# Two-layer convolution and attention kernel: the first residual's additions as accumulating on-chip transfers issued from GpSimd

## The chip, the cores and the metric

The kernel runs on one core of a Trainium2 chip. The metric is the device time of one execution in microseconds (us), lower is better. The engines are called as the profile calls them: PE (TensorE, matrix products), DVE (VectorE), ACT (ScalarE), POOL (GpSimd) and SP (SyncE, which here only issues transfers). Each takes its instructions in the order in which they were issued to it and waits on semaphores for the others.

## The reference: what is computed

The input is 16 images of 256 channels and 56 x 56 pixels, float32. Two layers follow one another, each added to its own input:

```python
# layer 0
x = x + _L0_conv_ref(_gn(x), ...)
# layer 1
x = x + _L1_conv_ref(_gn(x), ...)
```

`_gn` normalizes groups of 8 channels of an image to mean 0 and variance 1. Layer 0 takes the sign of that, makes three grouped 3 x 3 convolutions (4 groups of 64 channels, dilations 1, 3 and 5) with binarized weights, scales and rectifies each one, sums the three, and normalizes the sum over the 256 channels of each pixel. Layer 1 projects to queries, keys and values (8 heads of 8 channels), lets each pixel attend to its 3 x 3 neighbours with a learned and a fixed part, and projects back to 256 channels. The addition that the change touches is the first of the two `x + ...`.

## The kernel before

**Tiling.** An image's 28 upper and 28 lower rows lie side by side on 2 x 64 partitions for the signs. For everything after the convolutions an image is worked on in two strips, `u` 0 and 1. A strip has a tile for each of the four channel groups `g`: 128 partitions (two quarters of the rows x 64 channels) of 2 x 392 pixels, float32, so 784 elements or 3136 bytes per partition. `ct[g]` holds the group's layer-0 result, and `xt` holds the strip of the input, all four groups, and becomes the output in place.

**One strip of layer 0.** `conv` (L634) makes 36 products per group and dilation on PE (L644); ACT (L663, L670, L678), DVE (L673, L683) and POOL (L689) scale, rectify and sum them in `ct[g]`. `load_unit` (L1196) loads `xt` by four transfers from SP's queue (L1202). `channel_norm` (L721) follows: ACT squares (L727), PE sums over channels (L697) and spreads mean and root back (L711), DVE subtracts the mean (L755) and scales (L765), which also sums the result per partition. Then come the lines that the change is about, four times per strip, once per group: L778 adds `ct[g]` to `xt[:, g]`, and ACT's L782 squares the sum and collects the squares per partition in `sums`; it writes the squares over `ct[g]`.

**After both strips.** `fold` (L794) takes the statistics of the sum, from which layer 1's normalization follows: six small products on PE (L514, the group of that line with six products), some DVE and ACT steps, four POOL multiplications of the query, key and value weights (L803) and eight PE products (L825). Then `qkv` (L856) multiplies `xt` by these weights (L862), and `scores` (L906) and `attend` (L975) make the attention of each strip: POOL makes nine products per strip of queries and shifted keys (L915), PE sums them (L937), DVE and ACT and POOL make the softmax (L950 to L972), PE spreads it (L986), DVE multiplies with shifted values (L997), POOL adds these up (L1010, L1015 on DVE for the last), PE projects back (L1027), DVE adds to `xt` (L1037), and SP stores the strip (L1047).

**The next image's signs** are made meanwhile: SP loads each group twice into one of three `xh` buffers (L544), once for the statistics on ACT (L570) and once for the sign (L594); their statistics go through another L514, with two products. SP also copies 5 rows of signs across the two halves within the chip (`sgn<-sgn`, L606 and L607).

**What sets the order.** The program doesn't run these steps as they are written down. Each is an `Op` with the buffers it reads and writes; `Plan.emit` (L351) issues them by a hand-kept table of due times (`ORDER`, L80), one number per step and stage, with a period of 126.77 per image, as soon as the steps they depend on have been issued and a buffer is free. Steps of neighbouring images are so interleaved in every engine's queue. `either` (L492) puts a step on POOL, or on DVE where the table `ON_VECTOR` (L280) names it; for L778 that is so for three steps of the last image (stage `scale1$`). `pool` (L486) always puts it on POOL. Both count as one step, so that the due times of all steps stay with their steps. The buffers that matter here: 3 of `xt`, 7 of `ct`, 3 of `xh`, 3 of `m` (L1010), 5 of `p` (L915).

Of the kernel before, what the change touches and what calls it, by code (L numbers as in the profile page):

```python
# [11 lines left out]
ALU = mybir.AluOpType  # L12
# [281 lines left out]
class Plan:  # L294
# [16 lines left out]
    def op(self, engine, emit, r=(), w=(), hold=(), engines=()):  # L311


        k = self.noted.get((self.stage, self.image), 0)
        self.noted[self.stage, self.image] = k + 1
        if engines:
            emit = partial(emit, engines[k in ON_VECTOR.get(self.stage, ())])
        bufs = [k[0] if isinstance(k, tuple) else k for k in (*r, *w, *hold)]
        bufs = [k for k in dict.fromkeys(bufs) if isinstance(k, Buf)]
        o = Op(PERIOD * self.image + ORDER[self.stage][k], emit, bufs)  # L320
        for b in bufs:
            if not b.left and b.kind in self.queues:
                self.queues[b.kind].append(b)
            b.left += 1
        before = {}
        for k in r:
            for x in self.wrote.get(k, ()):
                before[id(x)] = x
        for k in w:
            for x in (*self.wrote.get(k, ()), *self.read.get(k, ())):  # L330
                before[id(x)] = x
        for k in r:
            self.read.setdefault(k, []).append(o)
        for k in w:
            self.wrote[k], self.read[k] = [o], []
        for x in before.values():
            x.after.append(o)
            o.wait += 1
        self.ops.append(o)
# [35 lines left out]
def preact_conv_attention(  # L375
# [16 lines left out]
    nc = tc.nc  # L392
# [84 lines left out]
    def pe(f, r, w, hold=()):  # L477
        op("PE", f, r, w, hold)

    def act(f, r, w):  # L480
        op("ACT", f, r, w)

    def dve(f, r, w):
        op("DVE", f, r, w)

    def pool(f, r, w):  # L486
        op("POOL", f, r, w)
# [4 lines left out]
    def either(f, r, w):  # L492

        op("POOL", f, r, w, engines=(nc.gpsimd, nc.vector))
# [199 lines left out]
    def lanes_sum(ps, bank, src, g):  # L694

        for i in range(NVB):
            nc.tensor.matmul(  # L697
                out=ps[i * LANES : (i + 1) * LANES, bank, 0:VB],
                lhsT=cm32,
                rhs=src[:, i // 2, i % 2 * VB : (i % 2 + 1) * VB],  # L700
                start=g == 0,
                stop=g == NG - 1,
            )

    def lanes_spread(ps, src):


        def f():
            for e in range(2):
                for h, q in ((0, 0), (1, 1), (0, 1), (1, 0)):  # L710
                    nc.tensor.matmul(  # L711
                        out=ps[q * GC : (q + 1) * GC, h, e * VB : (e + 1) * VB],
                        lhsT=bsel[e][q][h * GC : (h + 1) * GC],
                        rhs=src[h * GC : (h + 1) * GC, 0:VB],
                        start=True,
                        stop=True,
                    )

        pe(f, [src], [ps])

    def channel_norm(b, u, ct, xt, sums):  # L721

        ps = Buf("ps")
        for g in range(NG):
            plan.at(f"var{u}", b)
            sq = Buf("sq")
            act(lambda g=g, sq=sq: nc.scalar.activation(sq.tile, ct[g].tile, AF.Square), [ct[g]], [sq])  # L727

            def sum_of_both(g=g, sq=sq):
                lanes_sum(ps, 0, ct[g], g)  # L730
                lanes_sum(ps, 1, sq, g)

            pe(sum_of_both, [ct[g], sq], [ps])
        plan.at(f"root{u}", b)
        ms, t, s, r = (Buf("lv") for _ in range(4))


        mean, square = (lambda i=i: ps[:, i, 0:VB] for i in range(2))
        tt = nc.vector.tensor_tensor
        stt = nc.vector.scalar_tensor_tensor  # L740
        act(lambda: nc.scalar.copy(ms.tile, mean()), [ps], [ms])
        dve(lambda: tt(t.tile, mean(), ms.tile, ALU.mult), [ps, ms], [t])
        dve(lambda: stt(mean(), t.tile, -1.0, square(), ALU.mult, ALU.add), [t], [ps])
        dve(lambda: nc.vector.tensor_scalar(mean(), mean(), 0.0, EPS_LN, ALU.max, ALU.add), [], [ps])
        act(lambda: nc.scalar.activation(t.tile, mean(), AF.Ln), [ps], [t])
        act(lambda: nc.scalar.activation(square(), t.tile, AF.Exp, scale=-0.5), [t], [ps])
        act(lambda: nc.scalar.activation(s.tile, square(), AF.Square, scale=0.5**0.5), [ps], [s])
        dve(lambda: stt(t.tile, mean(), -1.0, s.tile, ALU.mult, ALU.mult), [ps, s], [t])
        dve(lambda: stt(r.tile, t.tile, 1.5, square(), ALU.add, ALU.mult), [t, ps], [r])
        plan.at(f"mean{u}", b)  # L750
        mb = Buf("ps")
        lanes_spread(mb, ms)
        for g in range(NG):
            dve(
                lambda g=g: nc.vector.tensor_tensor(ct[g].tile, ct[g].tile, mb[:, :, 0:SN], ALU.subtract),  # L755
                [mb],
                [ct[g]],
            )
        plan.at(f"root{u}", b)
        rb = Buf("ps")  # L760
        lanes_spread(rb, r)
        for g in range(NG):
            plan.at(f"scale{u}", b)
            dve(
                lambda g=g: nc.vector.scalar_tensor_tensor(  # L765
                    ct[g].tile,
                    ct[g].tile,
                    gam[:, g : g + 1],
                    rb[:, :, 0:SN],
                    ALU.mult,  # L770
                    ALU.mult,
                    accum_out=sums[:, g : g + 1],
                ),
                [rb],
                [ct[g], (sums, "sums")],
            )
            either(
                lambda e, g=g: e.tensor_tensor(xt[:, g], xt[:, g], ct[g].tile, ALU.add),  # L778
                [ct[g]],
                [(xt, g)])  # L780
            act(
                lambda g=g: nc.scalar.activation(  # L782
                    ct[g].tile,
                    xt[:, g],
                    AF.Square,
                    bias=bet[:, g : g + 1],
                    accum_out=sums[:, NG + g : NG + g + 1],
                ),
                [(xt, g)],
                [(sums, "squares"), ct[g]],  # L790
            )
# [420 lines left out]
    for b in range(NB):  # L1212
        sums = []
        xts = []
        for u in range(NU):
            ct = [Buf("ct") for _ in range(NG)]
            for g in range(NG):
                for d in range(3):
                    plan.at(f"conv{u}", b)
                    conv(b, u, g, d, ct[g])  # L1220
            plan.at(f"load{u}", b)
            xts.append(load_unit(b, u))
            sums.append(Buf("g"))
            channel_norm(b, u, ct, xts[u], sums[-1])
        before = sx
        if b + 1 < NB:
            sx = signs(b + 1)
        plan.at("fold", b)
        wf, bf = fold(before, sums)
        for u in range(NU):  # L1230
            for j in range(3):
                plan.at(f"qkv{u}", b)
                qkv(b, xts[u], wf, bf, j, u)
        for u in range(NU):
            at = scores(b, u)
            attend(b, u, at, xts[u])
# [114 lines left out]
```

## Time and profile before

| What | Value |
|---|---|
| Median of two runs | 2101.8 us (2094.55 and 2109.05) |
| The profiled execution | 2101.32 us |
| Its span, first to last instruction | 2099.5 us |
| Granted TensorE clock, mean | 0.935 of full speed |
| PE / DVE / ACT / POOL busy | 1798.0 / 1625.2 / 1292.8 / 1508.4 us |
| DMA engines, share of the span | 45.0% for SP's queue, 211.68 MB |
| L778 on POOL | 125 additions, 240.1 us, median 1.86 us |
| L778 on DVE | 3 additions, median 1.06 us |
| L782 on ACT | 128 squares, 121.1 us, idle before them 42.0 us |

How to read it. The page of a profile is one execution on the chip. "Busy" is the time in which an engine worked; instructions that only issue a transfer or wait are not counted in it. A group of instructions has a row of its own: the line of the program, engine, operation, what it writes `<-` what it reads, shapes, count `x`, then busy time in us and the mean of one in ns, then the time that the engine stood idle just before such instructions and what ended it (the releaser). The chain of work that ended last is followed back from the end, each time to what released an instruction. A timeline row has start and length in us, engine, line, operation, tiles, shapes and count, and in square brackets an idle time before it with its releaser. A row of the DMA issues ends with the size of a transfer and the median time from the start of its issue to its landing. A row of the waits gives who waited for whom, the total in us, how often, and the longest. Images and strips are counted from 0; from one image to the next the timeline advances by some 121 us (the first squares of the second strip start at 901.05, 1023.48, 1143.02 and 1265.15 us in images 6 to 9).

### The profile page before, as it was taken

Reading aid. Unit: us, or ns where it says so; the run is one execution under the profiler, and the core shown is the slowest. Engines: PE = TensorE matmul, PEld = TensorE weight load, DVE = VectorE, ACT = ScalarE, POOL = GpSimd, SP = SyncE. Lnnn points to the kernel's source line nnn. Section 1 sums busy time; section 2 is a strip of 40 time slices with the busy share of each in tenths; the row PEclk is TensorE's granted clock in tenths of the full one; section 3 lists DMA queues with packets and bytes.
Section 4 is the critical chain, followed back from the end, with each engine's and each line's share of the span. In section 5 each row is a group of like instructions: output and inputs, shape, how many; then the busy total and the mean of one; then the engine's idle time right before and its main releaser. Section 6 shows DMA issues by size and latency. Waiting matters only on the chain.

```text
span 2099.5 us, 71196 instructions
## 1 busy us (share of the span) xinstructions
PE 1798.0 (86%) x31770; PEld 906.3 (43%) x31770; DVE 1625.2 (77%) x2240; ACT 1292.8 (62%) x1733; POOL 1508.4 (72%) x884
## 2 busy tenths in 40 slices
PE   5667799898989989898989989898998989899694
PEld 4444254353535445353534435353443535344241
DVE  7565696968788696878879697877969687796876
ACT  6785575667667565767666576775757677463310
POOL 2233968878796887879597777968788786977714
PEclk8879999899999999999999999999999999999886
DMA  6760435535363654536364452637455353232212
GB/s 167 171 137 18 97 81 130 126 80 131 80 143 83 141 113 94 127 73 139 82 146 108 105 129 68 136 77 167 87 112 130 83 122 90 60 65 63 63 32 62
DMA packets 102420, 216.24 MB, mean 103 GB/s; under 512 B 10720, under 2 KB 84832, under 8 KB 102112
## 3 DMA queue, kind: packets, MB, share of 16 engines
q1 hardware_dynamic: 102112, 211.68, 45.0%
q8 instruction: 249, 4.08, 0.8%
q14 instruction: 59, 0.48, 0.1%
HBM read 154.85 MB, written 51.38 MB: 98 GB/s over the span
## 4 chain that ended last, share of the span: by engine, by line
PE 48%; DVE 27%; ACT 10%; issue 8%; POOL 4%; DMA 2%; SPq 0%; DVEq 0%; POOLq 0%; ACTq 0%
PE banks L644 16%; PE banks L862 12%; PE banks L937 7%; DVE m L997 5%; PE banks L986 4%; DVE xt L1037 4%; ACT xh L570 4%; PE banks L697 4%; DVE ct L765 3%; DVE ct L683 2%; ACT banks L678 2%; POOL m L1010 2%; DVE rl L683 2%; PE banks L1027 2%; DVE at L972 2%
## 5 line engine op out<-in xcount | busy, mean ns | idle before, releaser
L644 PE MATMUL banks<-sgn,wconv 64*64 64x392 bf16 x13824 | 674.3, 341 | 42.7 <-DVE rl L683 10.5
L1010 POOL TENSOR_TENSOR m<-m 128x784 f32<-128x784 f32 x252 | 469.7, 1864 | 169.1 <-DVE m L997 159.0
L644 PEld LDWEIGHTS <-wconv 64*64 64x64 bf16 x13824 | 441.5, 108 | 316.6 <-issue 144.4
L915 POOL TENSOR_TENSOR p<-qt,kt 128x784 f32<-128x784 f32 x273 | 473.1, 1768 | 108.8 <-PE banks L937 56.8
L678 ACT ACTIVATE banks<-banks,cbi,csc 128x784 f32<-128x784 f32 x384 | 373.0, 974 | 141.2 <-DVE ct L673 139.8
L689 POOL TENSOR_TENSOR ct<-ct,rl 128x784 f32<-128x784 f32 x128 | 237.9, 1859 | 247.0 <-DVE ct L683 99.9
L986 PE MATMUL banks<-at,wv 64*32 64x392 f32 x5120 | 315.6, 567 | 94.1 <-DVE m L997 49.9
L683 DVE SCALAR_TENSOR_TENSOR ct<-banks,oalpha,ct 128x784 f32<-128x784 f32 x256 | 262.0, 1028 | 84.9 <-ACT banks L678 82.7
L997 DVE TENSOR_TENSOR m<-banks,vt 128x784 f32<-128x784 f32 x288 | 274.6, 964 | 65.7 <-PE banks L986 59.3
L862 PE MATMUL banks<-xt,wf 64*64 64x392 f32 x3072 | 265.4, 495 | 3.9 <-DVE ct L755 3.9
L778 POOL TENSOR_TENSOR xt<-xt,ct 128x784 f32<-128x784 f32 x125 | 240.1, 1932 | 25.4 <-DVE ct L765 23.8
L937 PE MATMUL banks<-p,wk 32*64 32x392 f32 x4608 | 230.5, 499 | 11.7 <-POOL p L915 9.4
L673 DVE SCALAR_TENSOR_TENSOR ct<-banks,asc,ct 128x784 f32<-128x784 f32 x128 | 130.6, 1029 | 120.6 <-PE banks L644 117.1
L570 ACT ACTIVATE xh<-xh 128x1568 f32<-128x1568 f32 x120 | 180.9, 1508 | 7.2 <-DMA xh<-in_x 5.0
L986 PEld LDWEIGHTS banks<-at,wv 64*32 64x32 f32 x5120 | 67.3, 113 | 265.4 <-DVE m L997 106.1
L670 ACT ACTIVATE rl<-banks,asc 128x784 f32<-128x784 f32 x128 | 116.6, 911 | 103.6 <-POOL ct L689 59.1
L862 PEld LDWEIGHTS banks<-xt,wf 64*64 64x64 f32 x3072 | 114.3, 134 | 143.1 <-issue 131.0
L663 ACT ACTIVATE ct<-banks,mv,asc 128x784 f32<-128x784 f32 x128 | 128.3, 1003 | 49.1 <-PE banks L644 49.0
L683 DVE SCALAR_TENSOR_TENSOR rl<-banks,oalpha,rl 128x784 f32<-128x784 f32 x128 | 130.7, 1021 | 30.9 <-ACT banks L678 27.4
L1027 PE MATMUL banks<-m,wp 64*64 64x392 f32 x1024 | 116.2, 542 | 44.7 <-DVE xt L1037 24.7
L782 ACT ACTIVATE ct<-xt,pr 128x784 f32<-128x784 f32 x128 | 121.1, 947 | 42.0 <-POOL xt L778 34.3
L937 PEld LDWEIGHTS banks<-p,wk 32*64 32x64 f32 x4608 | 90.7, 131 | 118.4 <-issue 60.5
(111 smaller groups left out, 1961.8 us busy)
## 6 DMA issues: line engine op xcount, KB each, us to landing
xh<-in_x SPq DMA_DIRECT2D x248, 392.0 KB, 5.4
xt<-in_x SPq DMA_DIRECT2D x128, 392.0 KB, 7.0
out<-xt SPq DMA_DIRECT2D x128, 392.0 KB, 5.9
sgn<-sgn SPq DMA_DIRECT2D x128, 41.2 KB, 3.3
p<-in_w SPq DMA_DIRECT2D x12, 144.0 KB, 5.1
wq<-in_wqkv SPq DMA_DIRECT2D x1, 384.0 KB, 7.5
p<-in_wk_b SPq DMA_DIRECT2D x1, 320.0 KB, 6.9
p<-in_wk_c SPq DMA_DIRECT2D x1, 320.0 KB, 7.1
```

The costliest lines, as they stand in the source:

```text
L570: lambda func=func, col=col: nc.scalar.activation(inside(g) if b == 0 else image(xh), image(xh), func, accum_out=sums[:, col : col + 1]),
L644: nc.tensor.matmul(out=ps[q * GC : (q + 1) * GC, h, 0:SN], lhsT=wconv[h * GC : (h + 1) * GC, g, d, tap, :], rhs=sgn[g][h * GC : (h + 1) * ...
L678: lambda: nc.scalar.activation(n(), n(), AF.Relu, bias=cbi[:, g, s], scale=csc[:, g, s]),
L683: lambda: nc.vector.scalar_tensor_tensor(to.tile, n(), oalpha[:, g, s], to.tile, ALU.mult, ALU.add),
L689: lambda e: e.tensor_tensor(ct.tile, ct.tile, to.tile, ALU.add),
L778: lambda e, g=g: e.tensor_tensor(xt[:, g], xt[:, g], ct[g].tile, ALU.add),
L862: nc.tensor.matmul(out=ps[h * D : (h + 1) * D, q, 0:SN], lhsT=wf[q * GC : (q + 1) * GC, g, j, :], rhs=xt[q * GC : (q + 1) * GC, g, h, :], ...
L915: e.tensor_tensor(p.tile.rearrange("p x (r w) -> p x r w", w=W), _view(qt[:, 0, u * SN :], [(NU * SN + LANES, 2), (W, SR), (1, W)]), shift ...
L937: nc.tensor.matmul(out=ps[rt // 2][q * 64 : (q + 1) * 64, rt % 2, 0:n], lhsT=wk[r, j, :], rhs=rhs, start=s == 0, stop=s == 9,)
L986: nc.tensor.matmul(out=ps[rt * 32 : (rt + 1) * 32, q, 0:SN], lhsT=wv[q * 64 : (q + 1) * 64, j, :], rhs=at[q * 64 : (q + 1) * 64, rt, 0:SN] ...
L997: lambda j=j, m=m, ps=ps: nc.vector.tensor_tensor(m.tile.rearrange("p x (r w) -> p x r w", w=W), _view(ps[:, 0, :], [(512, 2), (W, SR), (1 ...
L1010: lambda e, m=m, acc=acc: e.tensor_tensor(acc.tile, acc.tile, m.tile, ALU.add),
```

## The change

In `channel_norm`, the addition of a group's result to the strip of the input is no longer an instruction of POOL (or DVE) but a transfer within the chip's memory, issued from POOL's queue, from `ct[g]` to `xt[:, g]`, that adds what it brings to what is there. One transfer has 128 partitions of 784 float32 elements, 392 KB. It reads and writes the same tiles, and the step keeps its place in the table of due times; the three steps of the last image that were DVE's are POOL's as well.

```diff
-            either(
-                lambda e, g=g: e.tensor_tensor(xt[:, g], xt[:, g], ct[g].tile, ALU.add),
+            pool(
+                lambda g=g: nc.gpsimd.dma_start(out=xt[:, g], in_=ct[g].tile, accum_op=ALU.add),
                 [ct[g]],
-                [(xt, g)])
+                [(xt, g)],
+            )
             act(
                 lambda g=g: nc.scalar.activation(
                     ct[g].tile,
```

## The prediction

> **What bounds the kernel now.** I read the busy shares first, then the chain of work that ended last, then the groups for the line that changes, and last the timelines of one steady image.
>
> ```profile
> PE 1798.0 (86%) x31770; PEld 906.3 (43%) x31770; DVE 1625.2 (77%) x2240; ACT 1292.8 (62%) x1733; POOL 1508.4 (72%) x884
> PE 48%; DVE 27%; ACT 10%; issue 8%; POOL 4%; DMA 2%; SPq 0%; DVEq 0%; POOLq 0%; ACTq 0%
> L778 POOL TENSOR_TENSOR xt<-xt,ct 128x784 f32<-128x784 f32 x125 | 240.1, 1932 | 25.4 <-DVE ct L765 23.8
> L782 ACT ACTIVATE ct<-xt,pr 128x784 f32<-128x784 f32 x128 | 121.1, 947 | 42.0 <-POOL xt L778 34.3
> ```
>
> PE is nearest to full, and POOL is only 4% of the chain. L778 is 240 us of POOL, but freeing POOL pays only where somebody waits for POOL. The second number to see is in the L782 row: ACT's square already waits for the add. So what counts is when the sum is *there*, not how long POOL is held.
>
> An image takes about 121 us. The timelines of POOL, ACT and PE at the second strip of image 6:
>
> ```profile
> 905.33 3.68 POOL L778 TENSOR_TENSOR xt<-xt,ct 128x784 f32<-128x784 f32 x2 [0.68 <-DVE ct L765]
> 907.80 0.96 ACT L782 ACTIVATE ct<-xt,pr 128x784 f32<-128x784 f32 x1
> 909.04 0.95 ACT L782 ACTIVATE ct<-xt,pr 128x784 f32<-128x784 f32 x1 [0.19 <-POOL xt L778]
> 908.45 1.74 PE L644 MATMUL banks<-sgn,wconv 64*64 64x392 bf16 x36
> 910.22 0.83 PE L514 MATMUL banks<-g,cst 128*128 128x8 f32 x6
> 911.16 6.38 PE L644 MATMUL banks<-sgn,wconv 64*64 64x392 bf16 x144
> ```
>
> The last two adds end at 909.01, the last square starts at 909.04, its sum is out at 910.08, and PE's fold product L514 starts at 910.22 with no idle time noted: just in time. PE takes its queue in order, so a later sum stops PE here. After it the 6.4 us of convolutions hide the rest of the fold, and PE runs without a gap to 957.
>
> The same views at the first strip of image 7, and the wait on PE that follows:
>
> ```profile
> 961.41 1.85 POOL L778 TENSOR_TENSOR xt<-xt,ct 128x784 f32<-128x784 f32 x1
> 963.30 0.95 ACT L782 ACTIVATE ct<-xt,pr 128x784 f32<-128x784 f32 x1
> 964.25 1.50 ACT L570 ACTIVATE xh<-xh 128x1568 f32<-128x1568 f32 x1
> 983.29 0.60 PE L514 MATMUL banks<-g,cst 128*128 128x8 f32 x2 [2.56 <-ACT xh L570]
> PE banks L514 <- ACT xh L570: 34.1, 9, 10.8
> ```
>
> The first square starts 0.04 us after its add. Behind it in ACT's queue stand the statistics of the next image (L570), and PE is already waiting for the last of them at 983.29. The other three squares of this strip stand far later (985.11, 987.39, 993.90), the middle two with some 14 to 18 us to spare.
>
> For the price of a transfer, the DMA issues of the page:
>
> ```profile
> xh<-in_x SPq DMA_DIRECT2D x248, 392.0 KB, 5.4
> sgn<-sgn SPq DMA_DIRECT2D x128, 41.2 KB, 3.3
> ```
>
> **What the Trainium skill says.** "DMA: Bandwidth & Descriptors", "SWDGE vs HWDGE vs iDMA": an accumulating transfer can only be issued by GpSimd, whose cores write its descriptors. Nothing is issued from POOL in this trace, so no run shows it yet. The same page, "Anatomy of one DMA": about 2.0 us fixed plus bytes at 436 GB/s; for 401,408 B that is an estimate of 2.9 us. The trace is slower for equal bytes: 5.4 us from issue to landing, 4.0 at best. "Collectives: The Full Stack", "The bandwidth ceiling: the fold count and why AG ≠ RS ≠ AR", says that a DMA addition needs two reads for each write; no run shows it. "SBUF — State Buffer", "Who interferes with whom": VectorE with two SBUF inputs and a reading GpSimd instruction block each other. The trace agrees: L962 takes 4.33 us at 948.79 beside POOL's products and 1.69 at 969.73; but those are L915's products, which stay.
>
> **The change part by part.**
>
> *Removed:* 125 adds on POOL, 240.1 us, and the last image's 3 on DVE (1.06 us median).
>
> *Added on POOL:* 128 issues. The trace has no such row. Lower bound 0.62 us (SP's median for an xt load); upper bound 1.86, the add itself, where POOL gains nothing. I take 1.2, the middle: 154 us. POOL gets back some 87 us, 0.66 each.
>
> *The wait on POOL* is for the same VectorE result (L765) and the same xt load as before, so what is queued behind it (L915's products, L1010's additions, L689) is held no longer by it. SP's queue is not passed and issues nothing new.
>
> *Added on the DMA engines:* 128 x 392 KB = 51 MB. The SP queue's 211.68 MB take 45% of the engines, so this is 11%, or 22% if the second read counts in full. In the stretch 957 to 1000 the engines are 51% busy already. I cost the delay of the xh loads at nothing: three buffers cover them. Without that cover L570 slips as the loads do (5 us of waits now).
>
> *The landing, T from start of issue.* Bounds: 3.0 (the skill's estimate without anything for issue or queues) and 9.0 (an xt load's 7.0, plus 2 for the second read in a busy stretch). I take 5.4, the xh load's own median for the same bytes: no HBM on the way, but a dearer issue and a second read. The halo copy's 3.3 us for a tenth of the bytes says that most is fixed.
>
> *Second strip.* POOL issues the third transfer at 905.33 and the fourth at 906.5. The fourth lands at 906.5 + 5.4 = 911.9; its square starts then and not at 909.04: **2.9 us late**, and so is L514. What comes late next is everything on PE, since from there to 957 PE has no gap to make it up. In about half of the images the square has 1.1 us of slack, but the first two squares (901.05 and 902.86, both right behind their adds) come late too and push ACT's queue by 2 us, which uses it up. 15 images x 2.9 = 43.5 us.
>
> *First strip.* The issue is at 961.41, the landing at 966.8 for 963.30: 3.5 late. ACT idles about 0.8 us soon after (for PE's L644), leaving 2.7 at L514. In 8 images PE waits there for ACT: 8 x 2.7 = 21.6. In 5 the timeline names DVE L997 instead; I allow ACT 1 us of slack: 5 x 1.7 = 8.5. Together 30 us.
>
> *Given back:* products that stand behind these adds on POOL come 0.66 earlier; PE waits for POOL's L915 at this place. I credit one per image, 14 x 0.66 = 9 us. The last image has its four adds on the chain (DVE L778, 2.6 us); four overlapping transfers against four adds I take as even.
>
> Sum: 43.5 + 30 - 9 = +65 us. The profiled execution took 2101.3 us (span 2099.5 and 1.8 around it), so **2166**; the median of the runs, 2101.8, is 0.5 off that. Each us of T is worth 15 + 13 = 28 us.
>
> **The rivals.**
>
> *Early landing.* T under 4.6 puts the loss under 42 us: within 2%. For it: an empty path without HBM, and the skill's 2.9. Against it: the halo's 3.3 for little data, and engines half busy. At T = 3.8 it gives 65 - 45 = +20, 2122.
>
> *Late landing.* Accumulation runs at half rate and gets half of busy engines, or pushes the xh loads: T above 7.3. At T = 8: 65 + 73 = +138, 2240. For it: the xt loads' 7.0. Against it: no HBM traffic of its own.
>
> *POOL was the bound.* POOL is busy 38.25 of 43 us in 957 to 1000 and PE waits there for its products: L937 for L915 29.2 and 9.4 us, for L778 6.4, L697 for L689 6.7, together 52 us. If an issue holds POOL under 1 us and T is at most 3.0, the loss is nil and nearly all of the 52 may come back: 2050. Against it: L997 hardly waits for POOL (6.1 us), and PE's other waits in that stretch are for DVE and ACT. Above T = 3.0 it decides nothing.
>
> *The transfer does not relieve POOL at all* (an issue as long as an add): 9 us of credit lost, and the fourth issue 0.7 later, 10 us: 2185. It lies inside the forecast's range.
>
> **How the numbers follow.** Forecast, T from 4.6 to 7.3: 2143 to 2219 by itself, chance 0.50. Late landing 0.15. Early landing, same within 2%, 0.28. POOL as bound, faster, 0.07. Two per cent, 42 us, is about what a measurement of this kernel tells from no change. Slower 0.65, same 0.28, faster 0.07. The range reaches over most of the early landing down to 2095, with POOL as bound and a little more left out below, and up to T = 8.4, 2250, with half of the late cases left out above.
>
> **What would show it.** Right: POOL's busy time falls to about 1270; L782's idle time, now 34 us for L778, becomes some 150 us or more and names a DMA; L514 with six products, at no idle in every image now, waits 2 to 4 us; the time from POOL's issue to landing reads 5 to 6. Wrong: L782 never waits for the DMA, or L514 stays at 0; then T was under 3 and the kernel is not slower. If the time grows but L514 doesn't, the loss came through the xh loads: L570 would then wait for DMA xh<-in_x. If ACT's lateness is taken up by gaps that I overlooked, 65 is too much.

## The result, and the profile after

The changed kernel takes 2232.0 us (2231.4 and 2232.6) where the kernel before takes 2101.8: a ratio of 1.062, 95% interval 1.046 to 1.078. The profiled execution's span is 2230.9 us, 131 more than before. The forecast was slower, at 2166 in a range of 2095 to 2250: the sign and the range hold, but the loss is twice the one worked out.

From the page after: the busy shares, the chain by engine, the groups of the transfers and of the squares, and the transfers' issue row. From L778 on, the changed kernel's lines stand one lower: L782 is L783 now.

```profile
PE 1841.3 (83%) x31770; PEld 920.7 (41%) x31770; DVE 1616.2 (72%) x2237; ACT 1289.7 (58%) x1733; POOL 1384.2 (62%) x887
PE 41%; DVE 17%; DMA 14%; ACT 12%; issue 9%; POOL 5%; SPq 1%; DVEq 0%; POOLq 0%; ACTq 0%
L783 ACT ACTIVATE ct<-xt,pr 128x784 f32<-128x784 f32 x128 | 120.8, 946 | 208.7 <-DMA xt<-ct 101.1
L778 POOL DMA_DIRECT2D xt<-ct x128 | 115.2, 922 | 50.5 <-DVE ct L765 44.3
xt<-ct POOLq DMA_DIRECT2D x128, 392.0 KB, 6.4
```

The DMA share of the chain has gone from 2% to 14% (8% of it are the new transfers). ACT's idle time before the squares has gone from 42 to 209 us. POOL's 1384 us now contain the 115 us of issues: its own work is down to 1269. And PE, which does the same 31770 products, is busy 43 us longer.

The timelines of POOL, ACT, DVE and PE at the second strip of image 6, the place whose rows the prediction showed (rows in between are left out):

```profile
959.79 0.86 POOL L778 DMA_DIRECT2D xt<-ct  x1
961.48 0.86 POOL L778 DMA_DIRECT2D xt<-ct  x1 [0.83 <-DVE ct L765]
966.20 1.81 POOL L778 DMA_DIRECT2D xt<-ct  x2 [1.20 <-DVE ct L765]
```

```profile
967.51 0.95 ACT L783 ACTIVATE ct<-xt,pr 128x784 f32<-128x784 f32 x1 [5.84 <-DVE ct L765]
970.04 0.95 ACT L783 ACTIVATE ct<-xt,pr 128x784 f32<-128x784 f32 x1 [1.49 <-DMA xt<-ct]
970.99 0.99 ACT L663 ACTIVATE ct<-banks,mv,asc 128x784 f32<-128x784 f32 x1
971.87 0.96 ACT L678 ACTIVATE banks<-banks,cbi,csc 128x784 f32<-128x784 f32 x1
974.45 0.95 ACT L783 ACTIVATE ct<-xt,pr 128x784 f32<-128x784 f32 x1
975.38 0.95 ACT L783 ACTIVATE ct<-xt,pr 128x784 f32<-128x784 f32 x1
```

Before, the first square of this strip had not waited at all, and the second one for 0.77 us:

```profile
902.86 0.95 ACT L782 ACTIVATE ct<-xt,pr 128x784 f32<-128x784 f32 x1 [0.77 <-POOL xt L778]
```

DVE and PE in the changed kernel:

```profile
972.87 1.03 DVE L683 SCALAR_TENSOR_TENSOR ct<-banks,oalpha,ct 128x784 f32<-128x784 f32 x1 [5.08 <-ACT banks L678]
```

```profile
973.96 3.14 PE L644 MATMUL banks<-sgn,wconv 64*64 64x392 bf16 x36 [3.74 <-DVE ct L683]
977.03 0.83 PE L514 MATMUL banks<-g,cst 128*128 128x8 f32 x6
```

Read them from the top. The first transfer is issued at 959.79, and its square starts 7.7 us later. (The releaser in the brackets, DVE L765, had ended at 958.3, before the issue; what came last is the landing, at 967.4.) The third and the fourth square don't wait, though the fourth is the one that the prediction watched: ACT is so late by then that their tiles have landed (at 971.9 and 973.7). What waits is everything behind the first two squares: ACT's L663 and L678 (with L670 the evictions: they take a convolution's result out of a bank of PSUM, PE's result memory), DVE's L683 behind L678, and PE's convolution behind L683, since its PSUM bank isn't free. L514 then follows with no wait of its own. From the end of the first scaling on DVE to L514 there were 12.5 us in the kernel before (897.7 to 910.2) and there are 18.7 now (958.3 to 977.0): 6.2 us in this image. Over images 1 to 13 the means are 12.8 and 18.2, so 5.4 us per image.

The same in the waits, first of the kernel before and then of the changed kernel:

```profile
DVE ct L683 <- ACT banks L678: 82.7, 88, 4.0
PE banks L644 <- DVE ct L683: 2.6, 4, 1.0
...
DVE ct L683 <- ACT banks L678: 197.0, 128, 8.4
PE banks L644 <- DVE ct L683: 63.7, 21, 4.8
```

The convolution at 973.96 also took 3.14 us, where 36 of these products take 1.74 elsewhere. Stretches of 5 us around it, whose last three columns are granted clock, DMA share and GB/s:

```profile
960.00:965.00 5.00, 3.03 (x40) 1.74 (x40) 4.93 (x8) 1.67 (x2) 3.35 (x3) 0.83 0.90 201
970.00:975.00 5.00, 1.26 (x20) 0.76 (x19) 2.02 (x3) 4.96 (x7) 0.00 (x0) 0.85 0.44 83
975.00:980.00 5.00, 5.00 (x86) 3.33 (x82) 4.40 (x9) 4.85 (x10) 1.50 (x1) 0.80 0.02 5
```

The kernel before had a clock of 1.00 in all four such stretches from 900 to 920, here the second:

```profile
905.00:910.00 5.00, 4.72 (x104) 3.32 (x96) 4.90 (x8) 4.81 (x9) 3.68 (x2) 1.00 0.00 0
```

The Trainium skill's "TensorE: Matmul & The Clock Gate", Part 1, says that PE's clock is halved after an idle window of about 3.4 us and restored after a busy one. The trace agrees in part: the granted clock is only ever full or half, and but for the last one the half stretches last 3.41 us or a multiple of it. They have become more, 57 (389 us together) where the kernel before had 40 (276 us), and the mean over the span fell from 0.935 to 0.913. But the window need not be idle throughout. The half stretch from 973.55 to 976.96 does follow 3.4 us almost without products; of the 57, only 10 do. Before the others PE stood idle for a part of the preceding 3.41 us, 2.4 us in the median of all 57 (by the trace's times of the products).

### The profile page after: what moved, and what is told of

Read it like the earlier page. It is cut to its first block, busy times and chain, and to the rows that moved or that the text cites. A ratio compares the mean times of both kernels' runs of the same rounds, so it can differ in the third digit from the quotient of the medians.

```text
span 2230.9 us, 71517 instructions
## 1 busy us (share of the span) xinstructions
PE 1841.3 (83%) x31770; PEld 920.7 (41%) x31770; DVE 1616.2 (72%) x2237; ACT 1289.7 (58%) x1733; POOL 1384.2 (62%) x887
## 3 DMA queue, kind: packets, MB, share of 16 engines
q0 software_dynamic: 18432, 51.39, 12.4%
## 4 chain that ended last, share of the span: by engine, by line
PE 41%; DVE 17%; DMA 14%; ACT 12%; issue 9%; POOL 5%; SPq 1%; DVEq 0%; POOLq 0%; ACTq 0%
PE banks L644 14%; PE banks L863 11%; DMA xt<-ct 8%; PE banks L938 6%; ACT xh L570 5%; PE banks L987 3%; DVE m L998 3%; ACT banks L678 3%; PE banks L697 3%; DMA xh<-in_x 3%; POOL m L1011 2%; DVE xt L1038 2%; DVE ct L683 2%; POOL p L916 1%; ACT ct L663 1%
## 5 line engine op out<-in xcount | busy, mean ns | idle before, releaser
L644 PE MATMUL banks<-sgn,wconv 64*64 64x392 bf16 x13824 | 710.2, 354 | 102.3 <-DVE ct L683 63.7
L644 PEld LDWEIGHTS <-wconv 64*64 64x64 bf16 x13824 | 450.8, 112 | 397.2 <-issue 211.5
L689 POOL TENSOR_TENSOR ct<-ct,rl 128x784 f32<-128x784 f32 x128 | 248.2, 1939 | 377.4 <-DVE g L526 120.1
L678 ACT ACTIVATE banks<-banks,cbi,csc 128x784 f32<-128x784 f32 x384 | 372.9, 973 | 132.6 <-DVE ct L673 131.2
L683 DVE SCALAR_TENSOR_TENSOR ct<-banks,oalpha,ct 128x784 f32<-128x784 f32 x256 | 262.3, 1029 | 198.8 <-ACT banks L678 197.0
L783 ACT ACTIVATE ct<-xt,pr 128x784 f32<-128x784 f32 x128 | 120.8, 946 | 208.7 <-DMA xt<-ct 101.1
L570 ACT ACTIVATE xh<-xh 128x1568 f32<-128x1568 f32 x120 | 180.7, 1506 | 8.9 <-DMA xh<-in_x 6.9
L670 ACT ACTIVATE rl<-banks,asc 128x784 f32<-128x784 f32 x128 | 116.4, 910 | 98.1 <-POOL ct L689 54.8
L683 DVE SCALAR_TENSOR_TENSOR rl<-banks,oalpha,rl 128x784 f32<-128x784 f32 x128 | 130.6, 1020 | 33.1 <-ACT banks L678 29.3
L778 POOL DMA_DIRECT2D xt<-ct x128 | 115.2, 922 | 50.5 <-DVE ct L765 44.3
L663 ACT ACTIVATE ct<-banks,mv,asc 128x784 f32<-128x784 f32 x128 | 127.9, 999 | 31.2 <-PE banks L644 30.8
```

The source lines that it names most:

```text
L570: lambda func=func, col=col: nc.scalar.activation(inside(g) if b == 0 else image(xh), image(xh), func, accum_out=sums[:, col : col + 1]),
L644: nc.tensor.matmul(out=ps[q * GC : (q + 1) * GC, h, 0:SN], lhsT=wconv[h * GC : (h + 1) * GC, g, d, tap, :], rhs=sgn[g][h * GC : (h + 1) * ...
L663: lambda: nc.scalar.activation(ct.tile, n(), AF.Identity, bias=mv2[:, g : g + 1], scale=asc[:, g, s]),
L678: lambda: nc.scalar.activation(n(), n(), AF.Relu, bias=cbi[:, g, s], scale=csc[:, g, s]),
L683: lambda: nc.vector.scalar_tensor_tensor(to.tile, n(), oalpha[:, g, s], to.tile, ALU.mult, ALU.add),
L689: lambda e: e.tensor_tensor(ct.tile, ct.tile, to.tile, ALU.add),
```

## The experiments

Ratios are to the kernel before on the same chip, with their 95% intervals; "us" are the differences of the medians. Three theories are told apart. Q: ACT's queue is held by the first two squares of the second strip, and the evictions behind them with it. F: the forecast's, the fourth square is late for the fold. C: the traffic costs, wherever it is.

| Run | Transfers | us | Ratio |
|---|---|---|---|
| changed kernel | all 128 | +130 | 1.062 (1.046 to 1.078) |
| e1 | second strip, 64 | +92 | 1.044 (1.040 to 1.049) |
| e2 | first strip, 64 | +30 | 1.014 (1.011 to 1.018) |
| e3 | second strip, first two, 32 | +96 | 1.047 (1.042 to 1.052) |
| e4 | second strip, last two, 32 | +51 | 1.025 (1.021 to 1.029) |
| e5 | all, plain copies | +106 | 1.051 (1.047 to 1.055) |
| e6 | none, additions left out | -6 | 0.996 (0.995 to 0.998) |
| e7 | first strip, middle two, 32 | +15 | 1.007 (1.005 to 1.009) |
| e8 | all, squares later, first try | +219 | 1.104 (1.101 to 1.107) |
| e9 | all, squares later, nothing else | +114 | 1.052 (1.045 to 1.059) |
| e10 | none, ACT held by 8 idle squares | +91 | 1.041 (1.036 to 1.047) |
| e11 | none, ACT held by 4 idle squares | +13 | 1.006 (1.004 to 1.008) |
| e12 | first strip, first one, 16 | +31 | 1.016 (1.014 to 1.019) |

**Which transfers cost: e1 to e4.** The transfer is made under a condition, else the addition stays. The diffs of e2, e3, e4, e7 and e12 are against e1.

```diff
+            if u == 1:
+                pool(
+                    lambda g=g: nc.gpsimd.dma_start(out=xt[:, g], in_=ct[g].tile, accum_op=ALU.add),
+                    [ct[g]],
+                    [(xt, g)],
+                )
+            else:
+                either(
...
```

e1: 

> Only the second strip's four additions (just ahead of the fold) are transfers; the first strip's stay POOL's. Theory Q (ACT's queue is held by the first two squares of this strip, and behind them the evictions that free PE's banks): about 95 us over the kernel before, near 2197, with PE L644 waiting for DVE ct L683. Theory F (the forecast's: only the fourth square is late, 3.9 us at a landing time of 6.4): 58 us, near 2160. Theory C (the traffic itself: each transfer costs the same wherever it is): half of the 130, near 2167.

```diff
-            if u == 1:
+            if u == 0:
```

e2: 

> Only the first strip's four additions are transfers. Theory Q: about 30 us over the kernel before, near 2131, through the first square and the statistics L570 behind it. Theory F: about 43 us, near 2145, at the same place. Theory C: 65 us, near 2167.

```diff
-            if u == 1:
+            if u == 1 and g < 2:
```

e3: 

> Only the first two additions of the second strip are transfers (32 of 128). Theory Q: nearly all of what the whole second strip costs, 80 to 95 us, near 2190. Theory F: next to nothing, since the fourth square is POOL's again, at most 10 us, 2112. Theory C: a quarter of the 130, 33 us, 2135.

```diff
-            if u == 1:
+            if u == 1 and g > 1:
```

e4: 

> Only the last two additions of the second strip are transfers (32 of 128). Theory Q with the fold waiting openly once ACT is no longer held earlier: 3 us per image, 45 us, near 2147, seen as a wait of PE L514 (six products) for ACT. Theory F: 58 us, near 2160, at the same place. Theory C: 33 us, 2135. If e3 and e4 add up to more than e1, the two latenesses hide each other.

e1 and e2 came out where Q put them, e3 just above what Q gave; e4's 51 us lie between Q's 45 and F's 58 and don't tell the two apart. A quarter of the transfers (e3) costs as much as the whole second strip (e1), so it isn't the traffic; another quarter (e4) costs half as much, so C's equal prices fall. F alone can't explain e3. But F's mechanism is real where it isn't covered: in e4 the fold's product (L514; the square is L789 in this kernel) waits for the square in every image, some 2.5 us, and the kernel pays 51 us. A row of e4's waits on PE:

```profile
PE banks L514 <- ACT ct L789: 39.8, 16, 3.7
```

e3 and e4 add up to 147 and together cost 92: the two latenesses hide each other.

**Is it the transfer or only its lateness: e10 and e11.** No transfers at all, the additions as in the kernel before, ACT kept busy instead.

```diff
...
+            def squares(g=g):
+                if u == 1 and g == 0:
+                    for _ in range(8):
+                        nc.scalar.activation(idle, idle, AF.Square)
...
```

e10: 

> The kernel before, with no transfer from POOL and all additions on POOL, and eight idle squares of a scratch tile (some 0.84 us each, 6.7 us) on ACT ahead of the first square of every second strip. Theory Q: ACT held at this place is all that the first two transfers do there, so this costs what e3 costs, 85 to 100 us: 2180 to 2200, with PE L644 waiting for DVE ct L683 some 60 us and a lower granted clock, near 0.92. If the transfers' traffic or POOL's issues carry e3's cost, this costs clearly less: under 2150.

```diff
-                    for _ in range(8):
+                    for _ in range(4):
```

e11: 

> As e10 with four idle squares (3.4 us). Theory Q with 0.8 us of ACT idle to take up first: about 2.6 us per image, 35 to 40 us if each us counts from there on, near 2132; if there is more slack behind it, less than half of e10's cost.

e10 costs 91 us, like e1 (92) and e3 (96), and PE's wait is like theirs (58.8 and 62.9 us; L646 and L685 are L644 and L683):

```profile
PE banks L646 <- DVE ct L685: 56.0, 18, 4.4
```

PE's busy time is 1836.7 us, again some 39 more than before, and the clock 0.919. So ACT held for 6.7 us at this place is enough; neither the traffic nor POOL is needed. Half of it (e11) costs 13 us, less than the 35 to 40 that I expected: by estimate there are some 2.5 us of slack (3.36 less 13/16). The other half costs 78 us, 1.45 us per us of hold and strip (78 over 16 x 3.36). What makes it more than 1 is in part PE's speed: its busy time is 1809.1 us in e11 and 1836.7 in e10, 28 us more for the same products, at clocks of 0.933 and 0.919.

**Taking the squares out of the way: e8 and e9.** Both keep all transfers.

```diff
-    kind("ct", UNIT, 7)
+    kind("ct", UNIT, 8)
...
-        117.05, 130.9, -162.12, -135.91, -2.52, 9.73, -728.7, -385.62, 138.26, 52.19, -389.71, -755.04,
+        117.05, 130.9, 138.24, -135.91, -2.52, 138.25, -728.7, -385.62, 138.26, 52.19, -389.71, -755.04,
```

e8: 

> The whole change, with the first two squares of the second strip put behind the next four evictions in ACT's queue, ahead of the third and fourth; an eighth ct buffer, since the tiles are held longer. No transfer is quicker by it. Theory Q: ACT no longer stands still with evictions behind it, PE's wait for DVE ct L683 (63.7 us) goes, and what stays is the fourth square's lateness and the first strip's: 2232 less 50 to 60, about 2175. If the cost is in the landing wherever the squares stand, no more than 15 us are won: above 2215.

It missed: 219 us slower than before. The eighth buffer let the planner change more than the two squares. Evictions, and the steps of DVE and POOL behind them, changed places in the queues as well, and PE stood waiting for the halo copy 14 times, where the changed kernel does so once, for 1.8 us. The row of e8:

```profile
PE banks L644 <- DMA sgn<-sgn: 35.4, 14, 2.9
```

These 35 us are only a part of what e8 lost beyond the changed kernel. So e8 says nothing on the squares alone. e9 takes the order from a dry run with seven buffers, moves only the two squares, and then issues in that order.

```diff
...
+        order = self.sequence()
+        for key, third in self.third.items():
+            for o in self.early[key]:
+                order.remove(o)
+                order.insert(order.index(third), o)
...
```

e9: 

> The whole change, and nothing moved in any engine's order but the first two squares of the second strip in 14 images: they stand directly ahead of the third, behind four evictions (an eighth ct buffer holds their tiles; all other queues are as in the changed kernel, which the kernel before this one did not keep). Theory Q: what e1 costs falls to what e4 costs, 45 us less than the changed kernel, 2180 to 2195, and PE's wait for DVE ct L683 falls from 63.7 us to under 15. If ACT's queue is not the way, 2215 or more.

The wait did what Q expected, the time did not: PE's wait for DVE falls from 63.7 to 12.6 us, but the median of 2215.6 lies where I had put the case against Q. Two rows of e9's waits on PE (L682 and L721 are L644 and L683, L552 is L514, L821 the square):

```profile
PE banks L552 <- ACT ct L821: 52.1, 15, 8.8
...
PE banks L682 <- DVE ct L721: 12.6, 7, 5.1
```

The wait has moved to the fold, at 3.5 us per image (11.9 us in the changed kernel, 52.1 here): with four squares in a row behind the landings, the fold's product waits instead of the convolution. Only 16 us are won, within the intervals of the two. So e9 shows that the order of ACT's queue decides who waits, not that another order saves the time; that a late ACT costs it is shown by e10. Whoever mends the first wait meets the second.

**What the landing is made of: e5.**

```diff
-                lambda g=g: nc.gpsimd.dma_start(out=xt[:, g], in_=ct[g].tile, accum_op=ALU.add),
+                lambda g=g: nc.gpsimd.dma_start(out=xt[:, g], in_=ct[g].tile),
```

> All 128 transfers are plain copies of the same tiles from POOL's queue; nothing is accumulated, so the first residual isn't added (the output is another one). If the accumulation (its second read) is what makes the landing late, the median from issue to landing falls from 6.4 to about 5 us, and at some 14 to 28 us of time per us of landing the kernel comes down by 20 to 40 us, to 2190 to 2210. If the lateness is what any transfer of this size issued here has, the landing stays within 0.5 us and the time within 15 us of 2232.

The issue row of e5 reads 4.8 us where the changed kernel's reads 6.4, and the time falls by 32 us between the medians, or 25 where each is set against the kernel before on its chip, both within the 20 to 40 expected. Of the 1.6 us, 0.3 are the issue itself, which holds POOL 0.56 us here and 0.87 there. For the rest see the queue rows: the same 51.39 MB keep the engines busy 7.5% of the span as plain copies,

```profile
q0 software_dynamic: 10240, 51.39, 7.5%
xt<-ct POOLq DMA_DIRECT2D x128, 392.0 KB, 4.8
```

and 12.4% with the addition:

```profile
q0 software_dynamic: 18432, 51.39, 12.4%
```

The plain copy is late too, and what is left goes with what else is under way. In the changed kernel a first transfer of a second strip, issued at 959.79 just after two xh loads (959.17), lands after 7.7 us; the last of a first strip, issued at 1059.01 with no other transfer just ahead of it, after 4.1. Over the 16 images the medians of these two places are 7.6 and 4.0. No run takes the loads away, so that they are the cause is argued from the places, not shown. The landing rows of the two transfers:

```profile
DMA to landing us min/median/max: 7.7/7.7/7.7
...
DMA to landing us min/median/max: 4.1/4.1/4.1
```

**What freeing POOL could bring at most: e6.**

```diff
-            either(
-                lambda e, g=g: e.tensor_tensor(xt[:, g], xt[:, g], ct[g].tile, ALU.add),
-                [ct[g]],
-                [(xt, g)])
+            pool(lambda: None, [ct[g]], [(xt, g)])
```

> The additions are left out altogether, with no transfer in their place (the output lacks the first residual): the most that freeing POOL of them can bring. Theory Q: POOL isn't the bound, but the squares no longer wait for an add, so a little less than before: 2070 to 2100. If POOL was the bound: 2050 or less.

6 us came, as Q expected. With this order of steps 0.2 to 0.5% is all that there is to have. POOL wasn't the bound, and no transfer, however quick, could have made this kernel clearly faster.

**Transfers for which nobody waits, and the one at the head of the statistics: e7 and e12.**

```diff
-            if u == 1:
+            if u == 0 and g in (1, 2):
```

e7: 

> Only the two middle additions of each first strip are transfers (32 of 128); their squares have 14 us or more to spare. Theory Q: nobody waits for them, POOL gets back some 1 us each: same as before within 1%, 2095 to 2115. Theory C (traffic): 33 us more, 2135. If POOL's relief is worth its time, 2080.

Their squares don't wait in the steady images, and still 15 us are lost, within the 1% expected but clear of noise. Two rows of e7's waits; before, they read 5.0 and 34.1 us:

```profile
ACT xh L570 <- DMA xh<-in_x: 22.1, 30, 2.5
...
PE banks L514 <- ACT xh L570: 72.2, 14, 10.9
```

Here it is the traffic, as far as these rows tell: the transfers go out among the xh loads, the statistics wait for these, and PE for the statistics.

```diff
-            if u == 1:
+            if u == 0 and g == 0:
```

e12: 

> Only the first addition of each first strip is a transfer (16 of 128), the one whose square stands ahead of the next image's statistics in ACT's queue. Theory F for this place: 2.7 us in 8 images and 1.7 in 5, about 30 us at a landing of 5.4; with the 4.5 us that this place shows in the changed kernel, about 18. With e7's 15 us beside it, what is left of e2's 30 to 42 us also makes this 15 to 27: 2110 to 2125. If the middle two carry all of e2, the same as before.

31 us, more than the 15 to 27 expected, with a landing of 5.7; ACT's squares wait 49.5 us for the transfer. But PE's wait for the statistics behind the square hasn't grown (31.5 us, and 34.1 before). What has grown is a wait in `attend` for DVE's L683, here in the kernel before and in e12 (L993 is L986):

```profile
PE banks L986 <- DVE ct L683: 28.2, 15, 3.5
...
PE banks L993 <- DVE ct L683: 46.4, 15, 4.9
```

So ACT's evictions are late behind this square too, as in the second strip. e7 and e12 add to 46 where e2, which holds both and a fourth transfer, costs 30. In e2 the statistics wait only 7.4 us for the xh loads: with ACT late already, the loads are in time. That these hide each other is read from the two waits; no run separates it further.

## Why the prediction was right or wrong

**Right: where the gain isn't.** POOL gives back more than I took (an issue holds it 0.87 us by its median, not 1.2; its own work fell to the 1269 us foreseen) and nobody is the faster for it. e6 bounds the rival "POOL was the bound" at 6 us. The 52 us of that rival were too many from the start: 29.2 and 6.4 of them are waits of weight loads, which overlap products. PE's own waits in that sum are 9.4 and 6.7 us, and all these waits are totals of the whole span, not of 957 to 1000.

**Right in size, only half in its path: the first strip.** 30 us were worked out for the first square ahead of the statistics; e12 gives 31, and the whole strip, e2, 30, at a landing of 5.7 us in e12 against 5.4. The loss does lie ahead of L514 with two products: from the strip's first scaling (L765) to it, images 2 to 12 take 26.9 us before and 29.1 in e12 by their means. But the sum let only the statistics be late. In e12 PE comes later as well, through the evictions behind the square (46.4 us for DVE's L683) and by 26 us of longer busy time (1824.0 against 1798.0), so its wait for the statistics stays as it was. What the statistics alone cost isn't separated. That the number came out so close is in part luck.

**Wrong: the second strip, 43.5 us, measured 92.** The step that failed is the sentence that the first two squares "come late too and push ACT's queue by 2 us, which uses it up". I let them only eat the slack of the fourth. They are the ones that cost: ACT stands still for 5.84 and 1.49 us, where before it stood for 0.77, with the evictions L663, L670 and L678 behind it, and PE waits for its banks 3.7 us. e3 shows it by itself, e10 without any transfer. The question that the prediction put to POOL's wait, what is queued behind the waiting instruction on its engine and who waits for that, it didn't put to ACT's. The price of the fourth square was not far off: e4 pays 51 us for the last two squares where nothing covers them.

**Wrong: T at that place.** 5.4 us was taken; the median is 6.4, and 7.7 and 8.5 for the two that count. The accumulation is not covered by "most is fixed": e5 puts 1.6 us of the median on it, 0.3 of them in the issue. Still, T doesn't explain the result: at 6.4 the prediction's own 28 us per us of T give 65 + 28 = 93 us, 2194. And T was one number for all places, where two xh loads are issued 0.6 us ahead of the first of these transfers.

**Wrong: PE's speed.** The sum took a wait as lost time and no more. PE's busy time grew by 43 us of the 131: L644 alone from 674.3 to 710.2 us, since products run at half clock behind stalls, as at 973.96. The same is seen in e10 (39 us) without any transfer. No run separates the clock from the stalls ahead of it.

**Wrong: what is given back.** The 9 us credited for the products behind the adds are in no run: e6, which leaves the additions out, gains 6 over the whole kernel, and e7, which shortens POOL at just this place, loses 15. The xh loads, costed at nothing under the cover of three buffers, are late once transfers are put among them (22.1 us of waits in e7, 5.0 before); in the changed kernel they are not (6.9), so this didn't decide here.

The parts: e1's 92 and e2's 30 make 122 of the 130. What is over is within the intervals; I leave it open. That 2232 lies in the range is luck in part as well: its upper end was there for landings of up to 8.4 us, and the median was 6.4.

Of the signs that the prediction named, POOL's 1270 came true (without the issues), and so did the squares' 150 us or more: 101.1 name the DMA and 51.4 a DVE L765 that had ended before, as at 967.51. The landing of 5 to 6 us did not (6.4), nor did L514 with six products waiting 2 to 4 us. For L514 at no wait the prediction had named two readings, a T under 3 with a kernel no slower, or a loss through the xh loads; neither holds (T is 6.4, L570 waits 6.9 us for the loads, 5.0 before). The loss went by a way that it had not listed.

## What to carry to other kernels

An operation moved from an engine to a transfer frees the engine and lengthens the latency; look first at what reads the result, and then at everything that stands behind the reader in its queue, not only at the last reader on the chain. If leaving the operation out altogether gains nothing in the same order of steps, there is nothing for moving it to gain there, and that is one run. And a stall on PE can cost more than its length: here the 36 products behind one of 3.74 us took 3.14 us instead of 1.74.

## What the runs showed of the hardware

- An accumulating transfer of 392 KB within the chip's memory took some 68% more of the DMA engines' time than a plain copy of the same tiles from the same queue (12.4% of 2230.9 us against 7.5% of 2194.8), and landed 6.4 against 4.8 us after the start of its issue (medians), 3.9 against 2.6 at best.
- Its issue held POOL 0.87 us by the median, less than half of the addition that it replaces (1.86). A plain copy's issue held it 0.56 us (e5).
- ACT held at one place for 3.4 us cost 13 us over 16 strips, for 6.7 us it cost 91.
- Of the changed kernel's 57 stretches at half clock 10 followed 3.41 us with hardly a product (3.3 us idle or more); in the median PE had been idle for 2.4 of the 3.41 us.
